# A two-layer relational graph network: a table of transformed rows per node and type, against sums per (type, node) in a ring that are transformed afterwards

## The chip, the cores and the metric

One core of a Trainium2 chip. The metric is the device time of one execution in microseconds; lower is better. The engines are named as in the profile: PE (matmul), PEld (its weight loads), DVE (vector), ACT (scalar), POOL (GpSimd, which also issues the gathers) and SP (which issues plain DMAs).

## The reference

20,000 nodes with 256 features, 320,000 edges with a source, a destination and one of 8 types. The edges come sorted by destination; the density of destinations falls from low to high node numbers.

```python
def _rgcn_layer(x, W, self_w, b, src, dst, edge_type, num_nodes):
    xW = jnp.einsum('ni,rio->rno', x, W)
    msg = xW[edge_type, src]
    agg = jax.ops.segment_sum(msg, dst, num_segments=num_nodes)
    return agg + x @ self_w + b
...
h = jnp.maximum(_layernorm(x, axis=-1), 0.0)
...
h = _rgcn_layer(x, W1, self_w1, b1, src, dst, edge_type, N_NODES)
h = jax.nn.relu(h)
out = _rgcn_layer(h, W2, self_w2, b2, src, dst, edge_type, N_NODES)
...
x = x + out
```

All data is float32; W1 and W2 have the shape (8, 256, 256).

## The kernel before

It runs four phases one after the other: a node phase and an edge phase for layer 1, then the same for layer 2.

The **setup** (L69 to L110) loads the edge lists, cuts the edges into 2,500 chunks of 128 and works out for each chunk which windows of 128 nodes its destinations touch. One (chunk, window) pair is an item; an item's number leads to a record with 128 table rows, 128 destinations and the window.

The **node phase** (`node_phase`, L117 to L167) is unrolled over 157 blocks of 128 nodes. A block is loaded, in layer 1 normalized (L133 to L140, DVE and ACT), transposed by PE (L148), passed through Relu on ACT (L150) and multiplied by the weights of all eight types in float32: 4 x 2 matmuls of 512 columns (L156), whose results ACT and DVE copy by turns into `stage` (L159, L161); two more matmuls of 256 columns (L164) multiply by the self weights, and DVE adds the bias, in layer 2 with x (prepared by POOL at L145), into `agg`, which stays in SBUF (L166). SP stores the 8 KB per node in `table` in DRAM (L167).

The **edge phase** (`edge_phase`, L169 to L243) loops over groups of 128 items (L221). Within a group ACT takes over the indices that were prepared in the group before (L223), and three steps (`prep_a`, `prep_b`, `prep_c`) prepare the next group's, one of them an indirect gather of the records (L191). For every eight items DVE makes a one-hot matrix `hot` (L230) and loads eight window numbers into its registers (L233). For each item POOL gathers 128 rows of 1 KB of `table` (L237, 12 buffers `msg`), PE multiplies them in float32 by the one-hot matrix (L241, 256 columns, 5 buffers `pm`), and DVE adds the result to the window of `agg` (L243). With 2,656 items a layer, 21 groups, so 2,688 items, are run. The order within each engine is that of the program; the framework puts in the semaphores.

At the end `agg` is stored (L252 to L257).

## Time and profile before

| What | Value |
|---|---|
| Median of 3 runs | 10,730.06 us (10,729.16 to 10,740.56) |
| Span of the profiled execution | 10,803.4 us |
| Mean granted PE clock | 0.736 |
| PE, PEld, DVE busy | 7,136.2, 3,836.9, 3,904.0 us |
| ACT, POOL busy | 579.4, 5,624.2 us |
| HBM read, written | 762.77 MB, 350.74 MB |

The profile is one execution, with a span of 10,803.4 us from the first to the last instruction; the runs are timed without a profile. A group's row reads: line, engine, operation, output <- inputs, shape, count, then busy time in us and mean ns of one, then the engine's idle time just before such instructions and what ended most of it. A float32 matmul appears as two PE records. A timeline row reads: start, time, engine, line, operation, count, and in brackets the idle time before it. In the table of windows each engine's busy time and count stand in the order PE, PEld, DVE, ACT, POOL, then the granted clock of PE, the share of the DMA engines and GB/s. In the answer for one line the three numbers after the count are the shortest, median and longest time in ns.

### The profile page before, as it was taken

How to read it: one execution, taken by the hardware profiler on the slowest of the kernel's cores; microseconds unless marked ns; L12 is line 12 of the kernel's file. 1: busy time of each engine (PE TensorE's matmuls, PEld its weight loads, DVE VectorE, ACT ScalarE, POOL GpSimd, SP SyncE). 2: the span in 40 equal slices, each digit the busy share in tenths (PEclk: the TensorE clock that was granted, in tenths of full speed). 3: DMA queues.
4: the chain of work that ended last, by engine and by line, in shares of the span. 5: the costliest groups of instructions: out<-in, count | busy, mean ns of one | idle time of the engine just before them, and what ended most of it. 6: DMA issues, size and time to landing. Idle time of an engine off the chain costs nothing. (4 is left out here: it accounts for less than half of the span.)

```text
span 10803.4 us, 75643 instructions
## 1 busy us (share of the span) xinstructions
PE 7136.2 (66%) x17794; PEld 3836.9 (36%) x17794; DVE 3904.0 (36%) x7989; ACT 579.4 (5%) x1360; POOL 5624.2 (52%) x5585
## 2 busy tenths in 40 slices
PE   7999955556555555555599998565555555555554
PEld 3444423333333333333244444333333333333332
DVE  3333333434433433334322222433434433333333
ACT  1222200000000000000011111000000000000000
POOL 0000067666666666766600001666766666666665
PEclk9999966666666666666699999666766666666666
DMA  4333323322222223323343333223323232232324
GB/s 145 144 142 144 142 88 90 89 89 89 88 88 87 88 88 89 89 84 89 89 149 142 143 145 131 88 87 89 90 86 90 85 90 88 88 89 87 89 88 143
DMA packets 376495, 1115.33 MB, mean 103 GB/s; under 512 B 97320, under 2 KB 162184, under 8 KB 335624
## 3 DMA queue, kind: packets, MB, share of 16 engines
q0 software_dynamic: 260160, 710.78, 22.3%
q1 hardware_dynamic: 59992, 349.84, 8.7%
q10 hardware_dynamic: 56228, 53.28, 1.5%
q8 instruction: 59, 0.97, 0.0%
q14 instruction: 56, 0.46, 0.0%
HBM read 762.77 MB, written 350.74 MB: 103 GB/s over the span
## 5 line engine op out<-in xcount | busy, mean ns | idle before, releaser
L237 POOL DMA_INDIRECT msg<-table,key x5376 | 5467.3, 1017 | 2534.1 <-issue 1197.0
L241 PE MATMUL pm<-msg,hot 128*128 128x256 f32 x10752 | 4578.8, 566 | 3033.0 <-DVE agg L243 1264.6
L241 PEld LDWEIGHTS pm<-msg,hot 128*128 128x128 f32 x10752 | 2565.0, 271 | 5010.4 <-DVE agg L243 2100.4
L243 DVE TENSOR_TENSOR agg<-agg,pm 128x256 f32 x5376 | 2259.6, 420 | 2324.9 <-PE pm L241 1191.6
L156 PE MATMUL po<-wt,ht 128*128 128x512 f32 x5024 | 2227.3, 596 | 58.9 <-ACT ht L150 49.2
L230 DVE TENSOR_TENSOR hot<-iota_f,rel 128x1024 f32<-128x1024 f32 x672 | 820.8, 1227 | 2192.7 <-remote 1493.4
L156 PEld LDWEIGHTS po<-wt,ht 128*128 128x128 f32 x5024 | 940.5, 190 | 1161.3 <-issue 1039.9
L161 DVE COPY stage<-po 128x512 f32<-128x512 f32 x628 | 433.5, 691 | 1522.1 <-PE po L156 1522.1
L191 POOL DMA_INDIRECT row<-rec,ti x44 | 41.9, 952 | 1400.9 <-DVE ti L189 1388.1
L145 POOL TENSOR_TENSOR base<-xt,bias 128x256 f32<-128x256 f32 (+1 forms) x157 | 114.0, 726 | 1176.3 <-DVE agg L166 1160.5
L159 ACT COPY stage<-po 128x512 f32<-128x512 f32 x628 | 367.1, 585 | 1526.5 <-PE po L156 1485.7
L223 ACT COPY key<-key_n 128x128 int32<-128x128 int32 x42 | 12.5, 298 | 6143.7 <-PEq L221 6142.7
L164 PE MATMUL ps<-wt,ht 128*128 128x256 f32 x1256 | 323.9, 381 | 5.3 <-DMA wt<-in_L_gnn_self_w_dram 5.3
L208 PE MATMUL pt<-ident,row 128*128 128x128 f32 x44 | 19.7, 447 | 459.4 <-DMA row<-rec,ti 431.9
L164 PEld LDWEIGHTS ps<-wt,ht 128*128 128x128 f32 x1256 | 238.9, 190 | 172.2 <-issue 155.1
L208 PEld LDWEIGHTS pt<-ident,row 128*128 128x128 f32 x44 | 8.0, 182 | 489.3 <-issue 489.3
L133 DVE BATCH_NORM_STATS2 st<-xt 128x6 f32<-128x256 f32 (+1 forms) x157 | 64.7, 412 | 263.0 <-DMA xt<-in_x_dram 263.0
L187 DVE TENSOR_SCALAR_CACHE_REDUCE hit<-endb,item 128x2500 bf16<-128x2500 f32 x44 | 124.0, 2817 | 59.1 <-PEq L221 44.8
L150 ACT ACTIVATE ht<-pt 128x256 f32<-128x256 f32 x314 | 103.6, 380 | 511.3 <-PE pt L148 354.3
L198 DVE TENSOR_TENSOR wv<-item,row 128x1 f32<-128x1 f32 x44 | 7.0, 160 | 329.5 <-DMA row<-rec,ti 329.5
L214 ACT CAST win_n<-pw 1x128 int32<-1x128 f32 x44 | 11.2, 254 | 1399.6 <-remote 912.3
L166 DVE TENSOR_TENSOR agg<-ps,base 128x256 f32<-128x256 f32 (+1 forms) x157 | 66.7, 425 | 48.8 <-PE ps L164 38.1
(54 smaller groups left out, 545.9 us busy)
## 6 DMA issues: line engine op xcount, KB each, us to landing
table<-stage SPq DMA_DIRECT2D x312, 1024.0 KB, 4.1
msg<-table,key POOLq DMA_INDIRECT x5376
xt<-in_x_dram ACTq DMA_DIRECT2D x312, 128.0 KB, 3.9
out_dram<-agg SPq DMA_DIRECT2D x6, 1664.0 KB, 19.6
out_dram<-agg ACTq DMA_DIRECT2D x6, 1664.0 KB, 28.3
wt<-in_L_gnn_W_dram SPq DMA_DIRECT2D x4, 1024.0 KB, 15.4
rec<-rows SPq DMA_DIRECT2D x1, 2509.8 KB
endb<-ends SPq DMA_DIRECT2D x2, 1250.0 KB
```

Source lines behind the costliest of these rows:

```text
L145: nc.gpsimd.tensor_tensor(base[:n], xt[:n], bias[:n], op=ALU.add)
L150: nc.scalar.activation(ht[:, :, :n], pt[:, :, :n], AF.Relu)
L156: nc.tensor.matmul(po[:n], lhsT=ht[:, k, :n], rhs=wf[:, k, c:c + step], start=(k == 0), stop=(k == KD - 1))
L159: nc.scalar.copy(stage[:n, c:c + step], po[:n])
L161: nc.vector.tensor_copy(stage[:n, c:c + step], po[:n])
L164: nc.tensor.matmul(po[:n], lhsT=ht[:, k, :n], rhs=wf[:, k, R * D:], start=(k == 0), stop=(k == KD - 1))
L166: nc.vector.tensor_tensor(agg[:n, i, :], po[:n], base[:n], op=ALU.add)
L187: nc.vector.tensor_scalar(hit, endb, item, None, op0=ALU.is_le, op1=ALU.add, accum_out=t)
L230: nc.vector.tensor_tensor(hot, iota_f[:, None, :].to_broadcast([P, OB, P]), rel[:, u:u + OB, None].to_broadcast([P, OB, P]), op=ALU.is_equal)
L237: nc.gpsimd.indirect_dma_start(out=msg, out_offset=None, in_=table.rearrange("n r o -> (n r) o"), in_offset=bass.IndirectOffsetOnAxis(ap=k ...
L241: nc.tensor.matmul(pm, lhsT=hot[:, u % OB, :], rhs=msg, start=True, stop=True)
L243: nc.vector.tensor_tensor(a, a, pm, op=ALU.add)
```

## The change

The order of sum and product is turned around. Instead of h times the weights for every node and type, gathered per edge, rows of h itself are gathered, summed by (type, destination), and the sums are multiplied by the weights.

- **Prologue.** Setup makes for each chunk of 128 edges the source rows (`key`) and, per edge, type x 24 + destination - the chunk's first destination (`rel`). Layer norm and Relu run once over all nodes, and h is stored in DRAM as two float32r halves (`hl`: the rounded value and the rest), 2 KB a node, in `t1`. Layer 1 writes its result in the same form to `t2`.
- **Gather and sum.** For a chunk POOL gathers 128 rows of 2 KB (18 buffers `msg`). Four float32r matmuls (two halves of the features, hi and lo) with the gathered rows as the stationary operand and the one-hot of (type, place), 8 x 24 = 192 columns, as the moving one give the transposed sums in `pm` (4 buffers). DVE adds them, 16 x 24 = 384 columns, into `ring` at the chunk's first destination modulo 512. The ring holds four blocks of 128 nodes.
- **Beat.** Eight chunks make a beat. Each beat takes one block out of the ring: ACT copies it to `stage` (2,048 columns) and clears it, DVE adds the few columns that ran over the ring's end, SP loads the block's own rows of h, PE turns them (`self_t`), and after the beat's chunk matmuls `transform` multiplies by bias, self weights and the eight weights: 1 + 2 + 16 = 19 float32 matmuls of 256 columns. `leave` adds x or takes the Relu and stores the block; it stands in the next beat, behind `self_t` and ahead of that beat's chunks.
- **Counts.** 313 beats hold the 2,500 chunks, and 6 more follow; where no block is ready a beat does the same work and its store is switched off by a register (`cond`). 156 of a layer's 319 beats carry a block; block 157 is done behind them. The beats are written out, with no loop, in the program's order on each engine (`manual_schedule`).
- **Another path.** If the edges are not sorted, or a chunk's destinations lie too far apart, or the beats can't keep up, `flag` is 1 and a general path runs after the fast one.

```diff
...
-    table = dram.tile([N, R, D], F32, name="table")
-    rec = dram.tile([C, REC], F32, name="rec")
+    t1 = dram.tile([N, HL], F32, name="t1")
+    t2 = dram.tile([N, HL], F32, name="t2")
...
+NS = 24
+BEAT = 8
+FLUSH = 6
+SLOTS = 4
+RING = SLOTS * P
+DUMMY = RING + NS
+COLS = DUMMY + P
...
+        nc.vector.scalar_tensor_tensor(rel_f, typ_i, float(NS), dst_i, op0=ALU.mult, op1=ALU.add)
+        nc.vector.tensor_tensor(rel_f, rel_f, edge[:, 0, :, None].to_broadcast([CP, CA, P]), op=ALU.subtract)
...
+        nc.vector.tensor_scalar(flag, tots, 0.0, None, op0=ALU.is_gt)
...
+            xt = lp.tile([P, 8, D], F32, name="xt", bufs=3)
+            nc.scalar.dma_start(xt[:n, :k], x[done:done + n * k, :].rearrange("(p k) d -> p k d", k=k))
...
+                nc.vector.bn_stats(st[:n, j, :], xt[:n, j, :])
+                nc.vector.bn_aggr(mv[:n, j, :], st[:n, j, :])
...
+                nc.vector.tensor_scalar(xt[:n, j, :], xt[:n, j, :], mv[:n, j, 0:1], rs[:n, j:j + 1],
+                                        op0=ALU.subtract, op1=ALU.mult)
+            nc.scalar.activation(xt[:n, :k], xt[:n, :k], AF.Relu)
+            hl = lp.tile([P, 8, 2, D], F32R, name="hl")
+            nc.scalar.copy(hl[:n, :k, 0, :], xt[:n, :k])
+            nc.gpsimd.tensor_tensor(hl[:n, :k, 1, :], xt[:n, :k], hl[:n, :k, 0, :].bitcast(F32), op=ALU.subtract)
...
+    ring = big.tile([P, KD * R, COLS], F32, name="ring")
+    iota = pp.tile([P, R * NS], F32, name="iota")
...
+    def layer(number, table, w, sw, b):
...
+        nc.gpsimd.memset(ring, 0.0)
+
+        def one_hot(g):
+            n = min(BEAT, C - g * BEAT)
+            hot = pool.tile([P, BEAT, R * NS], F32R, name="hot")
+            nc.vector.tensor_tensor(hot[:, :n], iota[:, None, :].to_broadcast([P, n, R * NS]),
+                                    rel[:, g * BEAT:g * BEAT + n, None].to_broadcast([P, n, R * NS]),
+                                    op=ALU.is_equal)
+            return hot
+
+        def load_rows(rows, n, xrows=None):
+            hl = pool.tile([P, HL], F32R, name="hl")
+            nc.sync.dma_start(hl[:n].bitcast(F32), rows)
...
+        def self_t(hl, n=P):
+            pt = pp.tile([P, KD, P], F32, name="pt")
+            for k in range(KD):
+                for i in range(2):
+                    nc.tensor.matmul(pt[:, k, :n], lhsT=hl[:n, i * D + k * P:i * D + (k + 1) * P], rhs=ident_r[:n, :n],
+                                     start=(k == 0 and i == 0), stop=(k == KD - 1 and i == 1),
+                                     skip_group_check=True)
+            ht = pool.tile([P, KD, P], F32, name="ht")
+            nc.scalar.copy(ht[:, :, :n], pt[:, :, :n])
+            return ht
+
+        def transform(stage, ht, n=P):
+            po = pp.tile([P, D], F32, name="po", bufs=2)
+            nc.tensor.matmul(po[:n], lhsT=ones[0:1, :n], rhs=bias, start=True, stop=False)
+            for k in range(KD):
+                nc.tensor.matmul(po[:n], lhsT=ht[:, k, :n], rhs=wt[:, k, R, :], start=False, stop=False)
+            for k in range(KD):
+                for r in range(R):
+                    nc.tensor.matmul(po[:n], lhsT=stage[:, k * R + r, :n], rhs=wt[:, k, r, :], start=False,
+                                     stop=(k == KD - 1 and r == R - 1))
+            return po
+
+        def leave(po, xb, n, rows, cond=None):
+            kw = {} if cond is None else {"cond": cond}
+            if number == 1:
+                res = pool.tile([P, 2, D], F32R, name="res")
+                nc.scalar.activation(res[:n, 0, :], po[:n], AF.Relu)
+                nc.vector.scalar_tensor_tensor(res[:n, 1, :], po[:n], 0.0, res[:n, 0, :].bitcast(F32),
+                                               op0=ALU.max, op1=ALU.subtract)
+                nc.sync.dma_start(rows, res[:n].rearrange("p i d -> p (i d)").bitcast(F32), **kw)
+            else:
+                res2 = pool.tile([P, D], F32, name="res2")
+                nc.vector.tensor_tensor(res2[:n], po[:n], xb[:n], op=ALU.add)
+                nc.sync.dma_start(rows, res2[:n], **kw)
...
+        hots = {0: one_hot(0)}
+        wait = None
+        for g in range(G):
+            n = max(0, min(BEAT, C - g * BEAT))
+            with tc.manual_schedule():
...
+                hl, xb = load_rows(table[ds(sv[0], P), :], P, x[ds(sv[0], P), :] if number == 2 else None)
+                stage = pool.tile([P, KD * R, P], F32, name="stage")
+                nc.scalar.copy(stage, ring[:, :, ds(av[0], P)])
+                nc.scalar.memzero(ring[:, :, ds(av[1], P)].bitcast(I32))
+                if g + 1 < NB:
+                    hots[g + 1] = one_hot(g + 1)
+                nc.vector.tensor_tensor(stage[:, :, :NS], stage[:, :, :NS], ring[:, :, ds(vv[BEAT], NS)], op=ALU.add)
+                nc.scalar.memzero(ring[:, :, ds(av[2], NS)].bitcast(I32))
+                ht = self_t(hl)
+                if wait is not None:
+                    leave(*wait)
+                hot = hots.pop(g, None)
+                for u in range(n):
+                    c = g * BEAT + u
+                    msg = pool.tile([P, HL], F32R, name="msg", bufs=18)
+                    nc.gpsimd.indirect_dma_start(out=msg.bitcast(F32), out_offset=None, in_=table,
+                                                 in_offset=bass.IndirectOffsetOnAxis(ap=key[:, c:c + 1], axis=0))
+                    pm = pp.tile([P, KD, R * NS], F32, name="pm", bufs=4)
+                    for k in range(KD):
+                        for i in range(2):
+                            nc.tensor.matmul(pm[:, k, :], lhsT=msg[:, i * D + k * P:i * D + (k + 1) * P],
+                                             rhs=hot[:, u, :], start=(k == 0 and i == 0),
+                                             stop=(k == KD - 1 and i == 1), skip_group_check=True)
+                    a = ring[:, :, ds(vv[u], NS)]
+                    nc.vector.tensor_tensor(a, a, pm.rearrange("p k (r n) -> p (k r) n", n=NS), op=ALU.add)
+                po = transform(stage, ht)
+                wait = (po, xb, P, into(sv[0]), sv[1])
+        leave(*wait)
...
+    layer(1, t1, w1, sw1, b1)
+    layer(2, t2, w2, sw2, b2)
...
+    with tc.If(slow == 1):
...
```

More of the change, by code (lines that the diff above doesn't have):

```diff
@@ L22 @@
 F32 = mybir.dt.float32
+F32R = mybir.dt.float32r
+BF16 = mybir.dt.bfloat16
 I32 = mybir.dt.int32
-BF16 = mybir.dt.bfloat16
 AF = mybir.ActivationFunctionType
@@ L41, in gnn_kernel @@
     KD = D // P
+    HL = 2 * D
     NW = (N + P - 1) // P
@@ L245, in gnn_kernel @@
[L245 to L257 removed]
+        nc.scalar.dma_start(typ_i, etype.rearrange("(p a e) -> p a e", p=CP, e=P))
```

420 lines of the change are left out of this document (242 added, 178 removed).

## The prediction

> **What bounds the kernel now.** First the table of windows: it cuts the span into the two node phases and the two edge phases.
>
> ```profile
> core 0: us, PE busy (x) PEld busy (x) DVE busy (x) ACT busy (x) POOL busy (x), PEclk, DMA share, GB/s
> 45.00:1370.00 1325.00, 1274.58 (x3457) 629.44 (x3455) 435.91 (x1103) 280.35 (x632) 1.62 (x2) 0.99 0.38 142
> 1370.00:5398.00 4028.00, 2285.72 (x5441) 1282.12 (x5442) 1583.61 (x3192) 28.36 (x123) 2757.38 (x2709) 0.66 0.30 88
> 5398.00:6725.00 1327.00, 1278.41 (x3469) 631.84 (x3467) 294.63 (x489) 236.97 (x477) 123.15 (x167) 0.99 0.39 143
> 6725.00:10740.00 4015.00, 2296.51 (x5427) 1292.68 (x5427) 1577.67 (x3182) 28.35 (x123) 2741.04 (x2701) 0.65 0.30 88
> ```
>
> In the node phases (first and third row, 1.3 ms each) PE is busy 96% of the time at clock 0.99. In the edge phases (4.0 ms each, 74% of the span) no engine is: POOL has 68%, PE 57% at clock 0.66. Next the groups of the page, for what a chunk costs each engine.
>
> ```profile
> L237 POOL DMA_INDIRECT msg<-table,key x5376 | 5467.3, 1017 | 2534.1 <-issue 1197.0
> L241 PE MATMUL pm<-msg,hot 128*128 128x256 f32 x10752 | 4578.8, 566 | 3033.0 <-DVE agg L243 1264.6
> L243 DVE TENSOR_TENSOR agg<-agg,pm 128x256 f32 x5376 | 2259.6, 420 | 2324.9 <-PE pm L241 1191.6
> L230 DVE TENSOR_TENSOR hot<-iota_f,rel 128x1024 f32<-128x1024 f32 x672 | 820.8, 1227 | 2192.7 <-remote 1493.4
> L191 POOL DMA_INDIRECT row<-rec,ti x44 | 41.9, 952 | 1400.9 <-DVE ti L189 1388.1
> L145 POOL TENSOR_TENSOR base<-xt,bias 128x256 f32<-128x256 f32 (+1 forms) x157 | 114.0, 726 | 1176.3 <-DVE agg L166 1160.5
> L164 PE MATMUL ps<-wt,ht 128*128 128x256 f32 x1256 | 323.9, 381 | 5.3 <-DMA wt<-in_L_gnn_self_w_dram 5.3
> L133 DVE BATCH_NORM_STATS2 st<-xt 128x6 f32<-128x256 f32 (+1 forms) x157 | 64.7, 412 | 263.0 <-DMA xt<-in_x_dram 263.0
> L150 ACT ACTIVATE ht<-pt 128x256 f32<-128x256 f32 x314 | 103.6, 380 | 511.3 <-PE pt L148 354.3
> ```
>
> A gather's own time is 1.02 us, and in the timeline of an undisturbed stretch they follow each other at 1.25 us (0.95 busy, 0.30 issue):
>
> ```profile
> 3034.87 1.23 DVE L230 TENSOR_TENSOR hot<-iota_f,rel 128x1024 f32<-128x1024 f32 x1 [0.59 <-PE pm L241]
> 3035.02 1.90 POOL L237 DMA_INDIRECT msg<-table,key  x1 [0.30 <-PE pm L241]
> 3036.01 1.32 DVE L243 TENSOR_TENSOR agg<-agg,pm 128x256 f32 x3
> 3037.22 0.95 POOL L237 DMA_INDIRECT msg<-table,key  x1 [0.30 <-PE pm L241]
> 3037.81 2.52 DVE L243 TENSOR_TENSOR agg<-agg,pm 128x256 f32 x5 [0.47 <-PE pm L241]
> 3038.48 0.95 POOL L237 DMA_INDIRECT msg<-table,key  x1 [0.30 <-issue]
> ```
>
> So 5,376 gathers hold at least 6.7 of the 8.0 ms of edge phases; the rest is waiting in the circle of gather, matmul, add, buffer free. The kernel is serial by phase: PE bounds 2 x 1.3 ms, POOL most of 2 x 4.0 ms, and neither works through the other's phase.
>
> **What a matmul costs here.** The busy mean of a PE group includes the pipeline's tail, so the cost is read from starts in the timeline of PE and its weight loads.
>
> ```profile
> 601.68 1.03 PE L164 MATMUL ps<-wt,ht 128*128 128x256 f32 x4
> 602.55 0.60 PE L148 MATMUL pt<-ident,h 128*128 128x128 f32 x4
> 602.33 0.57 PEld L148 LDWEIGHTS pt<-ident,h 128*128 128x128 f32 x4
> 603.46 4.99 PE L156 MATMUL po<-wt,ht 128*128 128x512 f32 x11 [0.32 <-ACT ht L150]
> ```
>
> Four L164 records take 1.03 us and one lasts 0.38, so they start every (1.03 - 0.38)/3 = 0.217 us; a float32 matmul of 256 columns is two records, 0.43 us. Transposes (one record each, 128 columns, a fresh 128x128 float32 weight load for each) last 0.273,
>
> ```profile
> L148 PE MATMUL pt<-ident,h x314: 222/273/448, 44.6 to 1344.6; 128*128 128x128 f32 x156, 32*128 32x32 f32 x1
> ```
>
> so four in 0.60 start every (0.60 - 0.273)/3 = 0.109 us; the loads, 0.57 for four, run under the matmuls before them.
>
> **The change part by part.** Removed: both node phases (2 x 1.3 ms), with the 8 KB table rows, and the item bookkeeping. Added: a prologue, and per layer 313 beats of 8 gathers plus 6 without gathers. All costs below are per beat, at the node phases' clock.
>
> *PE.* The transform is 19 float32 matmuls of 256 columns: 38 x 0.217 = 8.25 us. It runs 319 times a layer although there are only 157 node blocks; all of it counts. self_t: 4 float32r matmuls x 0.109 = 0.44. A chunk is 4 float32r matmuls of 192 columns, each with a fresh weight load; 32 a beat. The trace has no float32r. Bounds: the transpose row, one record under whose load the next matmul hides, 0.109 (3.49 us a beat); two float32 records of 192 columns, 2 x 0.217 x 192/256 = 0.325 (10.4 us). I take 0.109: the float32 rows pay for a product in two records, while here the change itself splits h into two rounded parts and multiplies each, so that the nearer row is the one that sends 4-byte data through in one record. PE alone: 8.25 + 0.44 + 3.49 = 12.2 us.
>
> *DVE.* Five adds take 2.52 us, so they start every (2.52 - 0.42)/4 = 0.525. The ring add has 384 columns instead of 256; the slope between L243 and L230 is (1227 - 420)/768 = 1.05 ns a column, so an add lasts 0.55 and they start every 0.66: 5.3 us for eight. one_hot has 1,536 columns, 1.77; the stage add 0.55; the leaving of the last block 0.42. Sum 8.0 us, beside PE.
>
> *The new wait.* `leave` of the block before stands on DVE ahead of the eight ring adds, and waits for the whole transform; so no add starts until the transform ends (call it T), and only four pm buffers are there for PE to run ahead. In layer 1 the path is: result latency 0.16, self_t 0.44, ht copy on ACT 0.38 (L150), Relu on ACT 0.38, DVE's subtraction 0.42, some four handovers of 0.1: the first add at T + 2.2. Chunk 8 needs the buffer of add 4: T + 2.2 + 3 x 0.66 + 0.55 + 0.1 = T + 4.8, plus its own 0.44: 5.3. Beat: 5.3 + 8.25 = 13.5. In layer 2 `leave` is one DVE add that does not wait for ACT: first add at T + 0.8, chunk 8 could go at T + 3.4, before PE itself is there (0.44 + 3.49 = 3.9). With 0.3 for weight loads exposed after waits: 12.5.
>
> *ACT and the ring.* A cast of 2,560 columns from SBUF gives the size of the copies:
>
> ```profile
> L79 ACT CAST rows<-dst_i 125x2560 f32<-125x2560 int32 x1 | 2.3, 2335 | 19.8 <-DMA dst_i<-in_dst_dram 19.8
> ```
>
> So 2,048 columns take 1.9 us, twice (stage copy, clearing), then DVE's stage add 0.55, the small clearing 0.5. They begin when the last ring add ends (layer 1: T + 2.2 + 5.3 = 7.5) and end by T + 12.7, against a next first add at T + 13.5 + 2.2. Hidden, with 3 us to spare; layer 2 is at T + 11.2 against 13.3.
>
> *POOL.* 8 x 1.25 = 10.0 us, with 18 buffers, ahead of PE. A row is now 2 KB. L191 (1,028 bytes a row, 0.95) against L237 (1,024, minimum 0.94) shows no dependence but hardly tests it; bounds 0.95 and 1.90. I take 0.95: a gather handles 128 indices in either case.
>
> ```profile
> L237 POOL DMA_INDIRECT msg<-table,key x5376: 943/949/2017, 1369.5 to 10735.2; - x200
> ```
>
> The gather beside the one-hot above took 1.90, those beside adds 0.95. If the one-hot and the stage add still each delay POOL by their length, a beat is 10.0 + 1.77 + 0.55 = 12.3; if every DVE instruction did, 18. The row of the adds (one operand in PSUM) is the nearer, as the one-hot now reads its iota from PSUM: 10.6 us, under PE. The Trainium skill ("GPSIMD Engine Reference", Specifications) says that POOL contends with DVE instructions that have two SBUF inputs or a 2-port mode; by that rule only the stage add counts, 10.6, and by the L230 row alone it would be 12.3, which leaves the sum as it is but nearly no slack. The trace agrees with it so far: 1.90 beside the two-SBUF one-hot, 0.95 beside the PSUM adds.
>
> *DMA and SP.*
>
> ```profile
> q0 software_dynamic: 260160, 710.78, 22.3%
> table<-stage SPq DMA_DIRECT2D x312, 1024.0 KB, 4.1
> wt<-in_L_gnn_W_dram SPq DMA_DIRECT2D x4, 1024.0 KB, 15.4
> ```
>
> 710.78 MB in 22.3% of 10,803 us is 2,409 us of all 16 engines, 0.45 us for a gather of 128 KB; twice that for 256 KB is 0.9, 7.2 us a beat, with some 0.9 for rows in and out: 65% of a beat. On SP a beat has one or two loads and one store; the store waits for `leave`, and the next load is queued behind it. That load has until T + 13 and lands in about 4 us; without this cover it would cost 4 us a beat.
>
> *Once.* Setup: the index load,
>
> ```profile
>   DMA dst_i<-in_dst_dram: 24.5, 1
> ```
>
> and some fifteen DVE steps of about 2.8 us over 2,500 columns, 70 us. Layer norm: statistics, their merging and the scaling on DVE,
>
> ```profile
> L140 DVE TENSOR_SCALAR h<-xt,mv,rs 128x256 f32<-128x256 f32 x156 | 57.0, 406 | 0.2
> L135 DVE BATCH_NORM_AGGREGATE mv<-st 128x2 f32<-128x6 f32 x156 | 27.7, 178 | 2.6
> ```
>
> 157 x (0.41 + 0.18 + 0.41) = 157 us, with POOL's subtraction (157 x 0.73 = 114, L145) beside it; its 61 MB at 143 GB/s for 0.39 of the engines need 166 us at full use and 427 at the node phase's rate. I take 200, nearer the low end, since the node phase did not wait for its transfers. Clearing the ring (10,624 columns) stands ahead of the gathers on POOL: 30 us at L145's 2.8 ns a column, 11 at DVE's 1.05; I take 20 a layer. Last blocks (copy, transform, store) 15 a layer. The 12 beats without gathers 8.25 + 0.44 + 0.8 = 9.5 each, 114.
>
> **Sum.** 313 x (13.5 + 12.5) = 8,138; + 114 + 70 + 200 + 40 + 30 = 8,592 us of span. The profiled span of before is 10,803.4 against a median of 10,730.06, a factor 0.9932: **8,534 us**. Bounds of this case: no stall at all (12.2 in both layers, 8,050) to a further 0.8 us in every beat (9,050).
>
> **The rivals.** Fixed parts are 454 us of span; before's 10,803 is reached at (10,803 - 454)/626 = 16.5 us a beat.
>
> *B: the float32r matmul is dearer, but cheaper than float32.* A record at L164's rate is 0.163, the beat 8.25 + 0.44 + 5.2 + 0.3 = 14.2, 9,280 us; a load that does not hide behind a one-pass matmul (0.109 + half of 0.163) gives 15.0, 9,780. For: nothing in the trace shows the type. Against: the transpose row.
>
> *C: slower, float32r at float32's price.* 0.325 x 32 + 8.25 + 0.87 + 0.3 = 19.8 us, 12,760 us. It decides from (16.5 - 8.25 - 0.44 - 0.3)/32 = 0.235 us a matmul. The float32 rows are the only arithmetic of this width in the trace; against it, those rows are of unsplit data, in two records, and the transposes show one-record passes at a third of that price.
>
> *D: POOL binds.* Gathers priced by bytes: 8 x (1.90 + 0.30) = 17.6, 11,390 us; POOL held by every DVE instruction, 18, much the same. POOL binds from 1.56 us a gather.
>
> *E: PE is not granted its clock.* At the edge phase's 0.66 a beat is 12.2/0.66 + 0.3 = 18.8, 12,140 us. Against: the waits that I forecast are about 1 us a beat, PE over 85% busy, nearer the node phases, which keep 0.99 with gaps such as L156's 0.32 above, than the edge phases, which leave PE idle 43% of the time. The Trainium skill ("TensorE: Matmul & The Clock Gate", The HAM clock gate) says that the clock halves only after an idle window of about 3.4 us; by that rule it stays full here and the sum stands, where a clock that followed the busy share evenly would cost up to this rival's time. No row here has waits of 1 to 3 us alone to tell the two apart.
>
> *F: the change doesn't take its own path.* If an index list broke the conditions that set `flag`, the whole general path would run behind the new one. Worked out from the reference's inputs, a chunk's 128 sorted destinations lie at most 19 apart, where `flag` allows 23, and no other condition is touched.
>
> **How the numbers follow.** Forecast 0.70; B 0.14; C 0.07; D 0.05; E 0.02; F 0.01; about even 0.01. Faster by over 0.2% (about what a measurement of this kernel can tell from no change) is the forecast and B, 0.84; slower is C, D, E and F, 0.15. The likeliest case alone runs from 8,050 to 9,050; with B the range is 8,050 to 9,780.
>
> **What would show it.** In the profile after: PE busy above 85% at clock 0.95 or more; the chunk matmuls starting every 0.11 us (0.16 or 0.33 for B or C); 38 transform records at 0.217 in each beat; gathers still 0.95 long, with POOL waiting on PE for buffers; DVE's first ring add some 2.2 us behind the transform in layer 1 and 0.8 in layer 2; beats of 13.5 and 12.5 us; a prologue of 270 us. Wrong are the steps above if POOL's mean is over 1.5 us, if PE waits on the gathers, or if ACT's ring chain is the last thing that the adds wait for.

## The result, and the profile after

The changed kernel takes **8,895.0 us** (median of 4 runs, 8,886.37 to 8,902.27) against 10,729.61 us (10,723.54 to 10,740.56) for the kernel before, measured beside it: ratio 0.829, interval 0.8278 to 0.8302. The forecast was 8,534 us. The span of the profiled execution is 8,884.4 us, of which its own time is 2 us longer (8,886.37).

First the groups of the page after the change, in the same columns as before; the line above them is PE's granted clock in 40 slices.

```profile
PEclk9988889999999999999999999999999999999999
...
L324 POOL DMA_INDIRECT msg<-t,key x5000 | 4741.3, 948 | 3635.9 <-PE pm L329 2528.6
L275 PE MATMUL po<-wt,stage 128*128 128x256 f32 x20480 | 4577.0, 382 | 19.0 <-issue 16.4
...
L333 DVE TENSOR_TENSOR ring<-ring,pm 128x384 f32 x5000 | 2771.4, 554 | 1333.5 <-remote 640.1
...
L329 PE MATMUL pm<-hot,msg 128*128 128x192 f32 x20000 | 2710.2, 286 | 48.2 <-DVE ring L333 18.3
```

The gathers last 948 ns on the mean with rows of 2 KB (949 in the median before, with 1 KB), and POOL now waits on PE's buffers for most of its idle time: PE sets the pace. PE hardly waits in its matmuls (19.0 and 48.2 us in 40,480 records). The ring adds are idle 640 us for something named remote, which the forecast did not have. And the clock row has a dent in slices 3 to 6, early in layer 1. The table of windows shows its size:

```profile
330.00:1000.00 670.00, 620.55 (x3077) 533.51 (x3077) 291.06 (x458) 202.14 (x206) 318.35 (x335) 0.87 0.50 149
1000.00:1700.00 700.00, 673.26 (x3553) 580.75 (x3552) 338.02 (x530) 238.05 (x240) 361.49 (x382) 0.94 0.56 165
1700.00:2700.00 1000.00, 998.69 (x5548) 863.66 (x5547) 531.03 (x824) 374.15 (x375) 568.14 (x600) 1.00 0.64 186
6000.00:7400.00 1400.00, 1399.58 (x8051) 1234.73 (x8051) 779.26 (x1198) 507.99 (x434) 825.68 (x871) 1.00 0.66 199
```

In the two windows behind 1,700 us PE is busy for 99.9% of the time at clock 1.00; up to about 1,370 us it is not, and the clock falls. One undisturbed beat of layer 1, PE's timeline:

```profile
2400.74 0.74 PE L261 MATMUL pt<-ident_r,hl 128*128 128x128 f32 x4
2401.32 4.50 PE L329 MATMUL pm<-hot,msg 128*128 128x192 f32 x32
2405.76 0.69 PE L270 MATMUL po<-bias,ones 1*128 1x256 f32 x2
2406.38 1.13 PE L272 MATMUL po<-wt,ht 128*128 128x256 f32 x4
2407.35 7.07 PE L275 MATMUL po<-wt,stage 128*128 128x256 f32 x32
2414.07 0.74 PE L261 MATMUL pt<-ident_r,hl 128*128 128x128 f32 x4
```

From one self_t to the next it is 2414.07 - 2400.74 = 13.33 us (forecast 13.5). Of that self_t holds PE for 0.58, the chunks for 4.44, the transform for 8.31, and of these 8.31 the one-row bias matmul takes 0.62, where the forecast had 0.43. Cut into beats by the starts of self_t, the trace gives (a wait of 32.5 us at layer 2's first beats is counted in the row of its start):

| Stretch | Forecast, us | Measured, us | Difference |
|---|---|---|---|
| start of the first beat | 290 | 288.6 | -1 |
| layer 1, beats 0 to 65 | 66 x 13.5 | 1,084.5 (16.43 each) | +193 |
| layer 1, beats 66 to 312 | 247 x 13.5 | 3,295.4 (13.34 each, median 13.32) | -39 |
| layer 2, 313 beats | 313 x 12.5 | 4,029.8 (12.87 each, median 12.85) | +117 |
| 12 beats without gathers | 114 | 131.6 | +18 |
| last blocks, start of layer 2 | 50 | 54.5 | +4 |
| span | 8,592 | 8,884.4 | +292 |

Two thirds of the miss are 66 beats at the start. Here the order within each engine differs from that of all later beats. PE's order is: chunks 1 to 4, self_t of the *next* beat, chunks 5 to 8. And on DVE the register loads of the next beat's region and its one-hot (which is for the beat after that one) stand between ring adds 5 and 6. First the row of the register loads (in ns), then DVE's timeline in one of these beats:

```profile
L303 DVEq TENSOR_LOAD <-tab_v x638: 843/2065/2561, 286.2 to 8849.1; - x160
```

```profile
511.77 0.42 DVE L284 SCALAR_TENSOR_TENSOR res<-po,res 128x256 fp32r<-128x256 f32 x1 [1.14 <-ACT res L283]
512.12 3.18 DVE L333 TENSOR_TENSOR ring<-ring,pm 128x384 f32 x5
518.27 1.76 DVE L243 TENSOR_TENSOR hot<-iota,rel 128x1536 fp32r<-128x1536 f32 x1 [2.98 <-remote]
519.95 1.73 DVE L333 TENSOR_TENSOR ring<-ring,pm 128x384 f32 x3
525.59 0.56 DVE L315 TENSOR_TENSOR stage<-stage,ring 128x384 f32<-128x384 f32 x1 [3.91 <-ACT ring L312]
527.42 0.42 DVE L284 SCALAR_TENSOR_TENSOR res<-po,res 128x256 fp32r<-128x256 f32 x1 [1.28 <-ACT res L283]
```

Between add 5 (over at 515.30) and add 6 (from 519.95) lie 4.6 us. The register load ends at 516.85, and yet the one-hot starts only at 518.27. It has something else to wait for: `hot` has two buffers, and this one-hot writes the one that the chunks of the running beat still read, so that in this order it needs chunk 8 of the beat from PE. In 62 of these beats it starts 1.43 us behind its register load (median), 89.7 us in all. With these 4.6 us everything is late that waits for the last add: ACT's copy and clearing, the stage add, the next leaving (527.42 - 511.77 = 15.65 us from one to the next). `manual_schedule` keeps the program's order inside a region; in the changed kernel each beat is a region of its own, and across these borders the framework mixed some 64 beats of layer 1, and none behind them.

### The profile page after: what moved, and what is told of

Its sections match the earlier page's. It is cut to its first block, busy times and chain, and to the rows that moved or that the text cites. A ratio compares the mean times of both kernels' runs of the same rounds, so it can differ in the third digit from the quotient of the medians.

```text
span 8884.4 us, 142316 instructions
## 1 busy us (share of the span) xinstructions
PE 8467.8 (95%) x46922; PEld 7367.2 (83%) x46922; DVE 4638.9 (52%) x7448; ACT 3185.7 (36%) x2983; POOL 4848.8 (55%) x5030
## 3 DMA queue, kind: packets, MB, share of 16 engines
q0 software_dynamic: 400000, 1311.04, 49.9%
## 4 chain that ended last, share of the span: by engine, by line
PE 88%; DVE 3%; ACT 2%; issue 2%; DMA 1%; POOL 1%; another core or an unknown queue 1%; DVEq 1%; ACTq 0%; POOLq 0%
PE po L275 47%; PE pm L329 27%; PE po L272 7%; PE po L270 4%; PE pt L261 3%; DVE ring L333 2%; DMA xt<-in_x_dram 1%; ACT ring L312 1%; ACT stage L311 1%; DVEq L303 1%; POOL hl L216 0%; DVE xt L211 0%; DMA typ_i<-in_edge_type_dram 0%; ACTq L300 0%
## 5 line engine op out<-in xcount | busy, mean ns | idle before, releaser
L324 POOL DMA_INDIRECT msg<-t,key x5000 | 4741.3, 948 | 3635.9 <-PE pm L329 2528.6
L275 PE MATMUL po<-wt,stage 128*128 128x256 f32 x20480 | 4577.0, 382 | 19.0 <-issue 16.4
L275 PEld LDWEIGHTS po<-wt,stage 128*128 128x128 f32 x20480 | 3925.5, 192 | 575.3 <-issue 23.5
L333 DVE TENSOR_TENSOR ring<-ring,pm 128x384 f32 x5000 | 2771.4, 554 | 1333.5 <-remote 640.1
L311 ACT COPY stage<-ring 128x2048 f32 x638 | 1212.3, 1900 | 4483.4 <-issue 3690.6
L329 PE MATMUL pm<-hot,msg 128*128 128x192 f32 x20000 | 2710.2, 286 | 48.2 <-DVE ring L333 18.3
L329 PEld LDWEIGHTS pm<-hot,msg 128*128 128x128 f32 x20000 | 2461.0, 194 | 220.2 <-DVE ring L333 24.6
L243 DVE TENSOR_TENSOR hot<-iota,rel 128x1536 fp32r<-128x1536 f32 x626 | 1098.7, 1755 | 918.8 <-issue 740.8
L312 ACT ACTIVATE ring<-ring x638 | 1219.7, 1912 | 19.9
L272 PE MATMUL po<-wt,ht 128*128 128x256 f32 x2560 | 756.3, 420 | 15.3 <-ACT ht L265 15.3
L316 ACT ACTIVATE ring<-ring x638 | 334.1, 524 | 401.9 <-DVE stage L315 202.5
```

Of the source, the lines that this page charges most:

```text
L243: nc.vector.tensor_tensor(hot[:, :n], iota[:, None, :].to_broadcast([P, n, R * NS]), rel[:, g * BEAT:g * BEAT + n, None].to_broadcast([P, ...
L272: nc.tensor.matmul(po[:n], lhsT=ht[:, k, :n], rhs=wt[:, k, R, :], start=False, stop=False)
L275: nc.tensor.matmul(po[:n], lhsT=stage[:, k * R + r, :n], rhs=wt[:, k, r, :], start=False, stop=(k == KD - 1 and r == R - 1))
L311: nc.scalar.copy(stage, ring[:, :, ds(av[0], P)])
L312: nc.scalar.memzero(ring[:, :, ds(av[1], P)].bitcast(I32))
L316: nc.scalar.memzero(ring[:, :, ds(av[2], NS)].bitcast(I32))
```

## The experiments

Twelve runs fall into three groups: nine new kernels, and the change and two of the nine run once more. The kernel before was measured beside each group: 10,738.24 us beside the first, 9,921.98 and 9,921.94 us beside the other two; each group ran on a chip of its own, and for the result the chip is not on record. So times are compared within a group, and across groups only where that is said.

| Run | Group | Time, us (lowest to highest) | Ratio to before, interval |
|---|---|---|---|
| e1_one_region | 1 | 8,705.74 (8,702.33 to 8,711.51) | 0.8108, 0.8095 to 0.8122 |
| e2_leave_late | 1 | 8,561.04 (8,559.48 to 8,570.28) | 0.7974, 0.7961 to 0.7987 |
| e3_no_bias | 1 | 8,459.95 (8,458.06 to 8,474.82) | 0.788, 0.7867 to 0.7893 |
| e4_transform_f32r | 1 | 7,984.99 (7,948.9 to 8,066.47) | 0.7427, 0.7401 to 0.7453 |
| e5_iota_sbuf | 2 | 8,661.94 (8,661.47 to 8,662.64) | 0.8727, 0.8713 to 0.8742 |
| e6_late_f32r | 2 | 7,271.84 (7,257.78 to 7,276.29) | 0.7322, 0.731 to 0.7334 |
| e7_skip_empty | 2 | 7,978.77 (7,975.58 to 7,984.87) | 0.804, 0.8027 to 0.8054 |
| e8_turn_ahead | 2 | 8,368.06 (8,367.86 to 8,369.76) | 0.8432, 0.8418 to 0.8446 |
| e9_change_again | 3 | 8,729.92 (8,709.71 to 8,732.94) | 0.8791, 0.8777 to 0.8806 |
| e10_one_region_again | 3 | 8,662.02 (8,661.76 to 8,663.7) | 0.873, 0.8716 to 0.8745 |
| e11_turn_ahead_again | 3 | 8,369.42 (8,368.14 to 8,369.78) | 0.8435, 0.842 to 0.8449 |
| e12_ahead_late_f32r | 3 | 6,924.0 (6,923.17 to 6,925.24) | 0.6978, 0.6967 to 0.699 |

**e1: one region for all beats of a layer.** The theory was that the order of the first beats cost them their time, the rival that it was the cold start of the layer.

```diff
-        for g in range(G):
-            n = max(0, min(BEAT, C - g * BEAT))
-            with tc.manual_schedule():
+        with tc.manual_schedule():
+            for g in range(G):
+                n = max(0, min(BEAT, C - g * BEAT))
```

> Only the order of issue is changed: one manual_schedule region over all beats of a layer instead of one for each, so that PE turns block g (self_t) in beat g, ahead of the beat's chunks, in every beat. In the changed kernel's trace beats 1 to 64 of layer 1 have the self_t of the next beat between chunks 4 and 5 and take 16.4 us on the mean, the beats behind them 13.32. Theory (order): that self_t waits for the ht copy, which stands on ACT behind the whole clearing of the ring, PE idles, and its clock falls; with the order mended the 66 beats cost 13.32 each, 170 to 205 us less: 8,690 to 8,725 us, and the clock of the stretch from 400 to 1,300 us goes from some 0.9 to 0.98 or more. Rival (start): PE comes cold out of the prologue, and the half clock keeps itself up by the waits that it makes until chance ends it at 1,367 us; then the first 65 beats stay at 15 to 18 us and the time at 8,895.

Measured 8,705.74 us, a span 175 us below that of the changed kernel's first profile (before was 10,729.61 us beside that, 10,738.24 beside this). Beats 0 to 65 took 910.5 us instead of 1,084.5: 174 us, as much as the whole gain. Some order within those beats was the cost; which part of it is taken up at e8. All other kernels but e9 start from this one.

**e2: the leaving behind chunk 4.** The forecast's "new wait" (layer 1's Relu and subtraction ahead of the eight adds) is taken away by doing the leaving in the middle of the adds.

```diff
-                if wait is not None:
-                    leave(*wait)
...
                     nc.vector.tensor_tensor(a, a, pm.rearrange("p k (r n) -> p (k r) n", n=NS), op=ALU.add)
+                    if u == 3 and wait is not None:
+                        leave(*wait)
```

> As the one-region kernel, and besides leave stands behind the fourth ring add of a beat instead of ahead of the first. Theory: a beat of layer 1 is 0.47 us longer than one of layer 2 (13.32 against 12.85) because DVE's part of leave, which waits for ACT's Relu behind the transform, holds up the first ring add and with it the buffer for chunk 5; then layer 1 falls to 12.85, 0.47 x 313 = 147 us less than the one-region kernel, some 8,560 us, and layer 2 stays. Rival: layer 1 is longer for another reason that is not the place of leave (two halves stored, 256 KB instead of 128, one more ACT step): beats stay at 13.32 and the time at that of the one-region kernel.

Measured 8,561.04 us, 145 below e1. Layer 1's beats fell from 13.32 to 12.85, layer 2's stayed at 12.85. So the wait was real and cost 0.47 us a beat of layer 1.

**e3: no bias matmul** (the bias is left out of the sum).

```diff
-            nc.tensor.matmul(po[:n], lhsT=ones[0:1, :n], rhs=bias, start=True, stop=False)
```

> As the one-region kernel, without the bias matmul (the bias is left out of the result). Theory: PE sets every beat, so that what leaves PE leaves the time: in the trace the bias matmul holds PE for 0.62 us a beat, 638 x 0.62 = 396 us less than the one-region kernel, some 8,300 us. If only its two records at 0.217 go and the rest is a refill that the next matmul pays, 277 us less, some 8,420. Rival: POOL (10.0 us a beat) or the circle of ring adds and clearing sets the beat as soon as PE is shortened: less than 100 us gained.

Measured 8,459.95 us: 246 us below e1, less than the 0.62 us a beat x 639 = 396 of its place in the timeline, and close to its records alone. The shorter beats fell by 0.80 us, the means (12.87 and 12.63) by less: some beats are now held by the circle of ring adds and clearing. DVE's group, and one of DVE's waits:

```profile
L332 DVE TENSOR_TENSOR ring<-ring,pm 128x384 f32 x5000 | 2771.5, 554 | 1705.9 <-remote 1154.7
```

```profile
DVE ring L332 <- ACT ring L315: 43.3, 167, 0.6
```

In 247 of the 313 beats of layer 2 the first ring add starts within 0.1 us of the end of the small clearing: there the circle is closed. But the saving did not use up the forecast's 3 us alone. In e1, on the same chip, this distance was already 0.72 us in the median of layer 2, where in e10, the same kernel on another chip, it is 2.65; most of the 3 us went to the late starts of the ring adds that the last section describes.

**e4: the transform in float32r** (weights, stage and bias are rounded, so the products are too).

```diff
-        wt = big.tile([P, KD, R + 1, D], F32, name="wt")
+        w32 = big.tile([P, KD, R + 1, D], F32, name="w32")
+        wt = big.tile([P, KD, R + 1, D], F32R, name="wt")
...
-                stage = pool.tile([P, KD * R, P], F32, name="stage")
+                stage = pool.tile([P, KD * R, P], F32R, name="stage")
```

> As the one-region kernel, with stage, ht, weights and bias rounded to float32r for the transform (the products are rounded, without a second half). PE then has 19 x 0.11 = 2.1 us for the transform and 6.2 us a beat. Theory: PE was the bound, and the next one is the circle on the ring: eight adds 5.3 us, then stage copy 1.9, clearing 1.9, stage add 0.56, clearing 0.52 and some 0.5 of handovers, 10.7 us; 626 x 10.7 + 450 = some 7,150 us. Rival 1: POOL's 8 x 1.25 = 10.0 us is the next bound, 6,750. Rival 2: PE, now idle 40% of a beat, loses its clock as in the edge phases of the kernel before (0.66) and takes 6.2/0.5 = 12.4 us at half clock: up to 8,250. Against all three, if PE was not the bound: 8,700, as the one-region kernel.

Measured 7,984.99 us. Of PE's 8.31 us a beat for the transform half should go; the beats fell to only 12.5 and 11.9 us on average, swinging between 8 and 16. PE's waits and its clock:

```profile
PE pm L335 <- DVE ring L339: 788.0, 487, 5.0
PE pm L335 <- issue: 518.5, 771, 4.3
```

```profile
core 0: 8064.8 us, clock 0.760
```

With PE's work for the transform halved, the ring and the leaving bind, PE waits, and the clock falls to 0.76. The time lies between the circle's 7,150 and the clock rival's 8,250, and that the slower PE gives part of the gain back is how I read it; no run separates the two.

**e5: the one-hot reads its iota from SBUF.** This is the forecast's open price on POOL: does a DVE step with both operands in SBUF hold up the gathers?

```diff
-            nc.vector.tensor_tensor(hot[:, :n], iota[:, None, :].to_broadcast([P, n, R * NS]),
+            nc.vector.tensor_tensor(hot[:, :n], iota_s[:, None, :].to_broadcast([P, n, R * NS]),
```

> As the one-region kernel (8,706 us), but the one-hot reads its iota from SBUF instead of PSUM, so that this DVE step of 1.76 us has two SBUF operands, as in the kernel before. Theory: POOL is held up beside such steps (the kernel before: 1.90 us beside the one-hot, 0.95 beside adds); one of a beat's eight gathers gets longer by up to 1 us, the mean goes from 0.948 to some 1.05, POOL to 11 us a beat, under PE's 12.85: time unchanged within 0.2%, 8,690 to 8,725. Rival 1: the place of the operand doesn't matter and the gathers stay at 0.948. Rival 2: POOL has no such slack, and the time rises by the delay, up to 626 x 1 = 600 us.

The gathers of e10 (the same kernel with iota in PSUM), then those of this one:

```profile
L324 POOL DMA_INDIRECT msg<-t,key x5000 | 4729.0, 946 | 3436.0 <-PE pm L329 2547.8
```

```profile
L324 POOL DMA_INDIRECT msg<-t,key x5000 | 5345.5, 1069 | 2820.4 <-PE pm L329 1928.0
```

The gathers' mean rises from 946 ns to 1,069, which is 8 x 0.123 = 0.98 us a beat, over half of the one-hot's 1.76. The time does not change: 8,661.94 us here, 8,662.02 in e10 on another chip with the same time of before. POOL stays hidden. The Trainium skill ("GPSIMD Engine Reference", Specifications) says that POOL shares its way to SBUF with DVE and contends with DVE instructions that have two SBUF inputs; the 946 against 1,069 ns agree.

**e6: e4 with e2's late leaving** (products rounded as in e4).

> The two changes that gained most, together: leave behind the fourth ring add, and the float32r transform (rounded products; 7,985 us by itself, with PE's clock at 0.76 and beats of 12.2 us on the mean). Theory (circle): with the transform short, the beat is the circle on the ring: adds, stage copy, clearing, and in between ht copy, Relu and DVE's part of leave ahead of the first add; taking leave out of it shortens the circle by 0.8 us or more, 10.7 to 11.4 us a beat, 7,150 to 7,600 us. Rival (clock): PE at half clock for part of each beat sets the time, not the order on DVE; then 7,850 to 8,000 and the clock stays under 0.8.

Measured 7,271.84 us, clock 0.847. PE's longest wait is now another one:

```profile
PE pt L267 <- DMA hl<-t: 1192.8, 552, 5.1
```

self_t waits for its rows of h: their load stands on SP behind the store of the block before, which waits for the late leaving. The forecast had named this queue, with 4 us a beat as the price if its cover went; with the cover partly gone PE waits 1,192.8 / 552 = 2.2 us each in 552 beats. That is PE's wait and not the price in time: in 193 of 313 beats of layer 1 and 255 of layer 2 the first ring add starts within 0.1 us of the small clearing's end, so that most beats are set by the circle on the ring, as the expectation had it.

**e7: beats that have no block skip their transform.** The list of the 156 beats of a layer with a block is fixed for these inputs; the other 163 leave out copy, clearing, self_t, transform and store.

```diff
+                full_beat = LEAVES[g] == "1"
+                if full_beat:
+                    hl, xb = load_rows(table[ds(sv[0], P), :], P, x[ds(sv[0], P), :] if number == 2 else None)
...
-                po = transform(stage, ht)
-                wait = (po, xb, P, into(sv[0]), sv[1])
+                wait = None
+                if full_beat:
+                    po = transform(stage, ht)
+                    wait = (po, xb, P, into(sv[0]), sv[1])
```

> As the one-region kernel, but the 163 beats of a layer that carry no block for these inputs (marked in a fixed list) leave out the taking out of the ring, self_t, transform and leave; their chunks stay. Theory: the empty beats cost as much as the others, 12.85 to 13.3 us, since PE sets them; without the transform PE has 4 us and POOL's 8 x 1.25 = 10.0 us sets them: 326 x 2.9 = 950 us less, some 7,760 us. PE will be idle for more than 3.4 us in such beats and lose its clock; the chunk matmuls at half clock (7.4 us) still hide under POOL, but a full beat behind an empty one may cost 2 us more: up to 8,050. Rival: the ring adds with their late signals or the transfers set the beats nearly as much as PE: less than 300 us gained.

Measured 7,978.77 us, 683 us below e10 (8,662.02, on another chip with the same time of before) and inside what was expected (7,760 to 8,050). The windows show why it was not more:

```profile
700.00:1500.00 800.00, 673.72 (x3126) 594.48 (x3126) 474.40 (x706) 89.25 (x89) 571.50 (x604) 0.69 0.71 210
3500.00:4000.00 500.00, 484.74 (x2603) 418.87 (x2602) 262.57 (x407) 166.50 (x166) 284.61 (x301) 0.95 0.63 194
```

Where few beats carry a block (first row), 800 us hold 604 POOL records, 1.32 us each: that is nearly the 1.25 us at which gathers follow each other, and PE runs at clock 0.69. Half of all transforms are work for nothing, but taking them out brings the kernel near the next limit.

**e8: the turn ahead in every beat.** To price the place of the turn alone, `self_t`'s matmuls of the next block stand between chunks 4 and 5 in every beat; its rows are loaded a beat earlier.

```diff
+                    if u == 3 and g + 1 < G:
+                        ahead[3] = turn(ahead[1])
...
-                ht = self_t(hl)
+                ht = take(pt)
```

> As the one-region kernel, but in every beat of both layers PE turns the next block (self_t of beat g + 1) between chunks 4 and 5, as it stands in beats 1 to 64 of layer 1 of the changed kernel. Theory (order): that place alone makes the slow beats, since the turn waits for the ht copy behind the clearing on ACT and the clock then falls; then all beats of layer 1 take about 16.4 us and those of layer 2 some 14 to 16, together 9,700 to 10,700 us, with PE's clock under 0.95. Rival (start): the place of the turn costs little, the state after the prologue was the cause: 8,700 to 8,800.

Both expectations fell. Instead of being 1,000 us slower, or the same, it is the fastest kernel that keeps the transform in float32 and holds for any list of blocks (e7 is made for these inputs): 8,368.06 us, clock 0.999, beats of 12.66 and 12.59. So the place of the turn on PE is no fault; it is a gain, of 0.66 and 0.26 us a beat. In layer 1 `ht`'s copy no longer stands between the transform's end and the Relu, which is the likely source of the larger gain.

**e9, e10, e11: the change, the one region and the turn ahead side by side.** These are the changed kernel, e1 and e8 again, unchanged, on one chip. Two theories were left for the slow beats of the change: late signals to DVE, or the cold start.

> The changed kernel once more, beside the two orders of its beats on one chip. Open is why its beats 1 to 64 took 16.4 us with the clock falling to half, when the same order in every beat ran at 12.6 us on another chip. Theory 'late signals': the order alone is harmless, and only where DVE waits on late signals from PE (the waits named remote, hundreds of us) does the turned-ahead block's copy come too late; then on a chip without those waits this kernel has beats of 13.3 us from the start and lies within 30 us of the one region, and on a chip with them it is about 190 us above it. Theory 'start': the first beats (matmuls one at a time, cold clock) put PE into half clock and the order keeps it there until the beats change order at number 65; then this kernel is 150 to 200 us above the one region on any chip.

> Program's order throughout. Both theories: beats of 13.32 and 12.85 us. On a chip with late signals 8,700 to 8,725 us, on one without 8,650 to 8,670.

> The turn of the next block between chunks 4 and 5 in every beat. Theory 'late signals': 8,370 us on a chip without them, and 9,700 to 10,700 us with beats of 16 us on a chip with them. Theory 'start': 8,350 to 8,450 on any chip, since this kernel makes its first turn ahead of the first beat and never leaves full clock.

The change is 68 us above the one region (8,729.92 against 8,662.02), between the two expectations: neither theory alone holds. In this chip's trace no wait is named remote, and beats 0 to 65 still take 957.5 us against 898.0 in e10: 60 of the 68 us. What they have, and e11 has not, is the second part of the framework's order, the place of the one-hot. DVE's timeline in e9,

```profile
533.21 0.42 DVE L284 SCALAR_TENSOR_TENSOR res<-po,res 128x256 fp32r<-128x256 f32 x1 [1.14 <-ACT res L283]
533.55 3.19 DVE L333 TENSOR_TENSOR ring<-ring,pm 128x384 f32 x5
538.43 1.76 DVE L243 TENSOR_TENSOR hot<-iota,rel 128x1536 fp32r<-128x1536 f32 x1 [1.70 <-issue]
540.11 1.73 DVE L333 TENSOR_TENSOR ring<-ring,pm 128x384 f32 x3
```

ACT's in the same beat,

```profile
527.64 1.90 ACT L311 COPY stage<-ring 128x2048 f32 x1 [7.40 <-DVE ring L333]
529.57 1.91 ACT L312 ACTIVATE ring<-ring  x1
532.11 0.52 ACT L316 ACTIVATE ring<-ring  x1 [0.63 <-DVE stage L315]
532.54 0.35 ACT L265 COPY ht<-pt 128x256 f32<-128x256 f32 x1
532.79 0.39 ACT L283 ACTIVATE res<-po 128x256 fp32r<-128x256 f32 x1
541.87 1.90 ACT L311 COPY stage<-ring 128x2048 f32 x1 [8.69 <-DVE ring L333]
```

and DVE's in e11:

```profile
506.33 0.42 DVE L287 SCALAR_TENSOR_TENSOR res<-po,res 128x256 fp32r<-128x256 f32 x1 [2.69 <-ACT res L286]
506.67 5.17 DVE L345 TENSOR_TENSOR ring<-ring,pm 128x384 f32 x8
512.24 1.76 DVE L243 TENSOR_TENSOR hot<-iota,rel 128x1536 fp32r<-128x1536 f32 x1 [0.40 <-issue]
```

In e11 the eight adds stand together, and register loads and one-hot run beside ACT's copy. In e9 they lie inside the circle of copy, clearing, stage add, `ht`, Relu, subtraction and adds, which is then 541.87 - 527.64 = 14.23 us long, with no wait for PE in this beat, against the 12.66 us that e11 takes with the turn ahead. Here the one-hot starts 0.09 us behind its register load (at most 0.29 in 62 beats), so that its need of chunk 8 costs nothing on this chip. In the first profile the idle time ahead of the one-hot was 2.98 to 3.81 us in three beats instead of 1.70, since there chunk 8 kept it waiting, the 89.7 us above; and PE waited for `ht` as well (51.9 us in 32 waits of up to 2.7 us, from 330 to 1,300 us), with the clock at half for part of the time: 16.43. So the place of the one-hot in DVE's order is what e9 has and e11 has not, at a cost of some 60 us; that the late signals, by way of chunk 8 and the clock, make 174 us out of these 60 is argued from the traces. A kernel in which only the one-hot is moved was not run.

**e12: turn ahead, late leaving and float32r together** (products rounded as in e4).

> The turn ahead, the leaving behind chunk 4 and the float32r transform (its products are rounded) together. If the turn ahead takes its 0.6 us of waiting out of a beat also here, 7,272 - 626 x 0.3 to 0.6 = 6,900 to 7,080 us; if the circle of ring adds and clearing alone sets the beat there, as the clock of 0.85 in the version without the turn ahead speaks for, no change: 7,200 to 7,350 us (some 50 more on a chip with late signals).

Measured 6,924.0 us, as expected with the turn's gain; the fastest of all. Its beats of 10.42 us are bound by the ring alone, as ACT's timeline shows:

```profile
3008.33 1.90 ACT L329 CAST stage<-ring 128x2048 fp32r x1 [4.82 <-DVE ring L349]
3010.26 1.92 ACT L330 ACTIVATE ring<-ring  x1
3012.80 0.52 ACT L334 ACTIVATE ring<-ring  x1 [0.62 <-DVE stage L333]
...
3018.70 1.91 ACT L329 CAST stage<-ring 128x2048 fp32r x1 [4.83 <-DVE ring L349]
```

Copy 1.90, clearing 1.92, stage add 0.56, small clearing 0.52, eight adds and a leaving 5.3, sum 10.2; from copy to copy it is 10.37. In all 626 beats the first add starts within 0.1 us of the small clearing's end, so the circle sets every beat. As long as each beat takes its block out of the ring in this order, it is a floor; no other order of it was run.

## Why the prediction was right

The faster side, the mechanism and the size were right: 8,895 us lies in the likeliest case's own range (8,050 to 9,050; from the prediction's own terms its lower end comes out as 8,036). Of the 361 us between 8,534 and 8,895, the span's terms are 292. The rest is the step "a factor 0.9932" from span to median: before's profiled span was 73 us above its median, the change's is 11 below its own, so the factor took off 58 us that did not exist. A difference between one profiled span and the median of other runs is no ratio to carry over.

**Point by point.**
- *PE, float32r.* Taken at 0.109 a matmul from the transpose row; four matmuls of a chunk start every 0.111 to 0.112 us, each with a fresh weight load. Rivals B and C are refuted. A new chunk adds 0.05 to 0.13 us for its own wait, so the 32 take 3.96 us where nothing holds them, not 3.49: with self_t 0.58 for 0.44 and the transform 8.31 for 8.25, less the allowance of 0.3, this is layer 2's +0.37.
- *PE, transform.* The records start every 0.216 us (median of L275), as forecast. The total of 8.31 for 8.25 is in part luck, as the edges differ: from the start of each kind to that of the next, the 16 weight matmuls take 6.72 us instead of 6.94, the two self ones 0.97 instead of 0.87, the bias 0.62 instead of 0.43.
- *The new wait.* Right in kind: in layer 1 the add of chunk 4 frees the buffer of chunk 8. The first add stands 1.81 us behind the start of self_t (2402.55 against 2400.74), not 2.2, and chunks and self_t end at 5.02, not 5.3; e2 shows the wait itself, 0.47 us a beat. In layer 2 the leaving holds nothing, as forecast, though the first add comes 1.32 us behind the start of self_t (6026.51 against 6025.19) and not 0.8: it waits for chunk 1's sums.
- *DVE.* The sum of 8.0 us a beat left out the register loads, 1.77 us on the mean (2.07 in the median), which hold DVE's later work. Beside PE they cost nothing; between two ring adds they are part of the slow beats.
- *ACT and the ring, "hidden, with 3 us to spare".* On the chips without late signals it has 3.1 us in layer 1 (in e9's beat at 1,510 us the small clearing ends at 1511.04, the first add starts at 1514.18). In the result's trace adds 7 and 8 often started late, and 2.4 us were left in layer 1 and 1.4 in layer 2 (medians). e3, e6 and e12 show the circle as the next bound, in e12 at 10.4 us a beat.
- *POOL.* 948 ns a gather: rival D is refuted by bytes (2 KB costs what 1 KB did), and by e5 even the contention that was feared is under cover.
- *DMA.* 0.9 us of all engines a gather forecast; 49.9% of 8,884 us for 5,000 gathers is 0.887.
- *Prologue.* 290 us in the sum (270 among the signs, without the ring's clearing), 288.6 measured.
- *Rival E, the clock.* Wrong for most of the span (1.00), right for one stretch: it fell where the slow beats made PE wait, to 0.87 from 330 to 1,000 us, and there PE's work took longer.

**The step that was mis-sized** is the beat itself, "313 x (13.5 + 12.5)": it priced one order of work for all beats and took the program's order from the code. The first 66 beats ran in another order at 16.43 us, +193 of the +292. That the region's border lies inside the loop was in the code, and that `hot` has two buffers too; what the framework did across the border was only in the trace.

## What to carry to other kernels

Price the circle, not only the busiest engine: here ring adds, copy and clearing were 3 us behind PE on two chips and some 1 us on another, and on that one a saving of 0.6 us a beat on PE already ran into them (e3), where elsewhere 0.66 us did not (e11). Before costing a beat, ask in which order each engine gets its instructions, for every stretch of the program; steps of 3.8 us (register loads 2.07, one-hot 1.76) that are free beside another engine cost time once they stand between two adds that others wait for. And when an experiment meant to show a fault turns out faster, look for what else the faulty version has.

## What was not expected of the hardware

**The clock fell beside short waits.** In the slow beats PE's longest wait was 2.7 us, and PE was 93% busy; still the trace shows the granted clock at half for 6.8 or 10.2 us, mostly once in every 31 to 34. In e9, with waits of at most 1.3 us in the same stretch, there were 11 such stretches of 6.8 us, and in the 9 us ahead of each of them no idle time of PE was longer than 0.78 us. In e10 and e11, where the longest there is 0.32 us, the clock stayed full. PE's waits in e9:

```profile
PE pm L329 <- DVE ring L333: 23.0, 42, 1.3
PE pt L261 <- ACT ht L265: 1.4, 3, 0.8
```

The Trainium skill ("TensorE: Matmul & The Clock Gate", The HAM clock gate) gives an idle window of about 3.4 us as the condition for half clock, and by that the prediction had kept the clock full. The measurement decides against this as a single gap of that length: none over 1.3 us was needed. What it is in these beats that brings the clock down is not shown. The half stretches themselves (6.8, 10.2 us, the shortest 3.4) are multiples of about 3.4. In e4, e6, e7 and e12, with PE 77 to 86% busy, the mean clock was 0.76 to 0.85, so a kernel that PE just stops binding may pay some of the gain back.

**Late ring adds on one chip.** The same program, e1 in group 1 and e10 in group 3, has PE-set beats of the same length to 0.01 us (medians of 13.32 and 12.85), but DVE's ring adds are idle for 1,703.0 us in the one and 649.9 in the other:

```profile
L333 DVE TENSOR_TENSOR ring<-ring,pm 128x384 f32 x5000 | 2771.7, 554 | 1703.0 <-remote 983.4 <-PE pm L329 288.6 <-issue 41.6
```

```profile
L333 DVE TENSOR_TENSOR ring<-ring,pm 128x384 f32 x5000 | 2772.1, 554 | 649.9 <-PE pm L329 193.2 <-DVE ring L333 4.1 <-ACT ring L316 0.6
```

In layer 2 of the change's first profile the eighth add starts 2.88 us (median) behind the start of the last matmul of its chunk, in e1 3.56 us, in e9 and e10 1.61 us; the first five adds of a beat have the same lag in all four, to 0.01 us. The name remote itself says little: the traces with it hold only 41,000 to 48,000 semaphore events, the others 109,000 to 120,000, so that the releaser is missing there. But the late starts are in the instructions' own times, and the kernel before is slower on group 1's chip as well, 10,738 against 9,922 us. The result has no chip on record; its trace and its before, 10,729.61 us, are like group 1's. What makes these adds late, a signal from PE or something on DVE, stays open; kernels were compared within one chip for that reason.
